# A cross-attention and Fourier FFN kernel: the FFN matrix built without folding the rows of W, its first sum over a quarter of the columns

## The chip, the core and the metric

The kernel runs on one NeuronCore of a Trainium2 chip. Its engines have a queue of instructions each and meet through semaphores: TensorE (matmuls; PE in the profile, PEld its weight loads), VectorE (DVE), ScalarE (ACT), GpSimd (POOL) and SyncE (SP), which here issues DMAs. The metric is the time of one execution on the device in microseconds (us). Before the change its median is 541.05 us over 3 runs (540.98 to 541.4).

## The reference

The input x has 2 x 2048 rows of 512. Each row goes through cross-attention (16 heads of 32, 128 keys per batch) and then through a linear layer that is given in the frequency domain:

```
x = x + attention(layernorm(x), ctx, mask) @ wo + bo
score = (q k^T / sqrt(32)) * mask;  score = -1e9 where score == 0;  softmax
w = complex(w_freq_real, w_freq_imag)          # 512 x 512
y = real(ifft(fft(layernorm(x)) @ w)) + bias
x = x + y
```

The two transforms and w are linear, so the second layer is one real matrix M (512 x 512), found once per call: M[n, m] is 1/512 times a sum over cosines and sines of n with the rows of w and of cosines and sines of m with its columns. All arithmetic is float32.

## The kernel before

The 4096 rows of x are 8 groups of 512, each of four tiles of 128 rows. Group i, tile t is a slot: scores of 16 heads (128 x 128 each), softmax in two halves of eight heads, transposes of the weights, and between them a part of another group's work, so that TensorE always has a matmul to do: queries of the next group (`q`), context (`c`) and projection (`o`) of the last, FFN (`y`) of the last or the one before. The order of all queues is written out by hand: every engine takes its instructions in the program's order. Groups 1 to 7 run in a regular pattern of slots; group 0 has a prologue of its own, up to about 97 us with the first slot of group 1, in which M is also made. The change touches this prologue and the first slots of group 1.

The steps that the change and the prediction speak of:

- `relative` (L234) subtracts a row's first element, `query_statistics` (L209 to L214) takes mean and variance on VectorE and the inverse deviation on GpSimd, `query_norm` (L217, VectorE) normalizes in place, `query_transposes` (L186 on TensorE, L188 on ScalarE) turns the tile. The rows of group n are prepared while group n - 1 or n - 2 is in its slots.
- `Queries` (L200) is a chain of four matmuls of 512 columns (384 for the rest of group 0), evicted by ScalarE (L293) in `evict`.
- `Softmax`: `masked` (L334: scores times mask, VectorE), `maxima` (L341 turns zero scores into the masked value, L343 takes the minima, L344 scales them; VectorE), `exponentials` (eight L350 on ScalarE), `divided` (the reciprocal L362 on VectorE, the multiplication L363 on GpSimd).
- `transposed_weights` (L380 on TensorE) turns weights of four heads into one bank; ScalarE (L387) or, where it is told to, VectorE (L385) copies them out.
- `Values` (L200, evicted by L584 on VectorE) makes v of one batch.
- The matrix M. Its two inputs wr and wi (real and imaginary part of w) are loaded to two tiles. `FoldRows` uses the symmetry of cosine and sine in the rows: a matmul with the flipped identity (`flip`, L614) mirrors a block of 128 rows, and VectorE adds it to and subtracts it from its mirror image (L621, L624), row 0 and row 256 apart (L623, L626). There are four folds, two each for wr and wi. `fold_columns` does the same with columns, on GpSimd (L645, L646), into `cols`. `Mirrored` then sums over 257 cosines and 255 sines (L685) and builds the 512 outputs out of the two halves with an add and a subtraction (L706, L707): four times as `h` (into `half`) and four times as `m` (into `m_ffn`). What belongs to the first row comes in as a bias (`first_rows`: a transpose, L669, of rows that small DMAs, L663, have gathered).

PSUM, where TensorE writes, has three pools of two tiles: scores (`ps_sc`), transposes (`ps_tp`) and chains (`ps_mm`, used by queries, values, folds, h, m, context and projections). A chain's first matmul waits until the chain before the last one has been evicted. In SBUF, wr and wi lie in the two buffers that hold the residual rows of x later, and the cosines and sines in one of the buffers for transposed weights. The order of the prologue's calls stands at the foot of the builder, from `evict_biases, evict_keys = keys()` on.

Of the kernel before, what the change touches and what calls it, by code (L numbers as in the profile page):

```python
# [22 lines left out]
def kernel(  # L23
# [76 lines left out]
    flip = const_tile([P, P], "flip")  # L100
    nc.vector.tensor_copy(flip, ident[:, P - 1 :: -1])
# [55 lines left out]

    wr = big_tile("x", 2, "wr")
    wi = big_tile("x", 2, "wi")
    row0 = const_tile([1, 2, D], "row0")  # L160
    nc.sync.dma_start(row0[:, 0, :], wf_re[0:1, :])
    nc.sync.dma_start(row0[:, 1, :], wf_im[0:1, :])
    nc.sync.dma_start(wr[:, :HC, :], chunks(wf_re[1 : HD + 1, :]))
    nc.sync.dma_start(wr[:, HC:, :], chunks(wf_re[HD:, :]))
    nc.sync.dma_start(wi[:, :HC, :], chunks(wf_im[1 : HD + 1, :]))
    nc.sync.dma_start(wi[:, HC:, :], chunks(wf_im[HD:, :]))
# [4 lines left out]
    nc.sync.dma_start(dft[:, :HC, :], chunks(dft_cos[HD:, :]))  # L171
    nc.sync.dma_start(dft[:, HC:, :], chunks(dft_sin[HD:, :]))
# [23 lines left out]
    def chain(name, lhs, rhs, width=D, between=()):  # L196

        ps = ps_mm.tile([P, D], FP, tag="mm", name=name)[:, :width]
        for c in range(NC):
            nc.tensor.matmul(  # L200
                ps, lhs(c), rhs(c), start=(c == 0), stop=(c == NC - 1)
            )
            if c == HC - 1:
                call(between)
        return ps
# [69 lines left out]
    class Queries:  # L275


        def __init__(self, i, g, first=0):
            self.i, self.g, self.first = i, g, first

        def pe(self):
            i, g = self.i, self.g
            if i not in qTs:
# [5 lines left out]
                width=GQ - self.first * P,  # L289
            )  # L290
# [307 lines left out]
    m_ffn = const_tile([P, NC, D], "m_ffn")  # L598
    half = big_tile("pt", 6, "half")
    cols = big.tile([P, 4, HC, HD], FP, tag="cT", bufs=1, name="cols")  # L600

    class FoldRows:
# [3 lines left out]
        def __init__(self, name, t, other, sign, c):  # L606
            self.name, self.t, self.other, self.sign = name, t, other, sign
            self.c = c

        def pe(self):  # L610

            t, c = self.t, self.c
            self.low = ps_mm.tile([P, D], FP, tag="mm", name=f"low_{self.name}_{c}")
            nc.tensor.matmul(  # L614
                self.low, flip, t[:, HC - 1 - c, :], start=True, stop=True
            )

        def evict(self):
            t, c = self.t, self.c
            total, high = t[:, HC - 1 - c, :], t[:, HC + c, :]  # L620
            nc.vector.tensor_tensor(total, self.low, high, ALU.add)  # L621
            if c == 0:
                nc.vector.tensor_copy(total[0:1, :], high[0:1, :])  # L623
            nc.vector.tensor_tensor(high, high, self.low, ALU.subtract)  # L624
            if c == 0:
                nc.vector.tensor_scalar(  # L626
                    high[0:1, :], row0[:, self.other, :], self.sign, None, ALU.mult
                )

        on_vector = True  # L630

    def fold_columns():


        up, down = slice(HD + 1, D), slice(HD - 1, 0, -1)
        rp, rm, ip, im = wr[:, :HC, :], wr[:, HC:, :], wi[:, :HC, :], wi[:, HC:, :]
        for k, (x1, x2, op, first) in enumerate(
            (
                (rp[:, :, up], rp[:, :, down], ALU.add, rp[:, :, HD : HD + 1]),
                (im[:, :, up], im[:, :, down], ALU.add, im[:, :, HD : HD + 1]),  # L640
                (ip[:, :, down], ip[:, :, up], ALU.subtract, rp[:, :, 0:1]),
                (rm[:, :, up], rm[:, :, down], ALU.subtract, im[:, :, 0:1]),
            )
        ):
            nc.gpsimd.tensor_tensor(cols[:, k, :, 1:], x1, x2, op)  # L645
            nc.gpsimd.tensor_copy(cols[:, k, :, 0:1], first)  # L646

    def cols_of(what, g):
        return lambda i: cols[
            :,  # L650
            2 * what + i // HC,
            HC - 1 - i if i < HC else i - HC,
            g * P : (g + 1) * P,
        ]
# [11 lines left out]
    def first_rows(name, rows, scale):  # L666
# [4 lines left out]
        nc.scalar.mul(add, ps, scale)  # L671
        return add

    class Mirrored:
# [3 lines left out]
        def __init__(self, name, lhs, dst, scale):  # L678
            self.name, self.lhs, self.dst, self.scale = name, lhs, dst, scale

        def pe(self):
            ps = ps_mm.tile([P, D], FP, tag="mm", name=self.name)
            self.even, self.odd = ps[:, : HD + 1], ps[:, HD + 1 :]
            for i in range(NC):
# [3 lines left out]
                    dft[:, i, : HD + 1] if i < HC else dft[:, i, 1:HD],  # L688
# [4 lines left out]
        def evict(self, add, eng=nc.gpsimd):  # L693
            low, high = self.dst[:, 1:HD], self.dst[:, D - 1 : HD : -1]
            nc.scalar.activation(
                self.dst[:, : HD + 1],
                self.even,
                AF.Identity,
                bias=add,
                scale=self.scale,  # L700
            )
            odd = self.odd
            if eng is nc.gpsimd:
                odd = work.tile([P, HD - 1], FP, tag="odd", name=f"odd_{self.name}")
                nc.scalar.mul(odd, self.odd, self.scale)
# [112 lines left out]
    for t in range(TG):  # L818
        relative(1, t, nc.gpsimd if t < 2 else nc.vector)
    query_statistics(1, 0, TG - 1)  # L820
    for g in range(NC):
        first_queries(0, g)
# [4 lines left out]
    folds = [  # L827
        FoldRows(name, w, other, sign, c)
# [397 lines left out]
```

## Time and profile before

| what | value |
|---|---|
| median of 3 runs | 541.05 us (540.98 to 541.4) |
| the profiled execution | 541.23 us, its span 539.0 us |
| granted TensorE clock, mean | 1.000 |
| TensorE idle, 20 to 99 us | 4.6 of 79 us |
| VectorE busy, 20 to 99 us | 64.9 of 79 us |
| ScalarE busy, 20 to 99 us | 53.8 of 79 us |
| GpSimd busy, 20 to 99 us | 50.4 of 79 us |
| start of the scores of slots (0,1), (0,2), (0,3), (1,0) | 36.45, 50.36, 63.96, 80.88 us |

A group of instructions is one source line on one engine with one pair of tiles; behind its name stand the number of instructions, the busy time in us, the mean of one in ns, and the idle time before them with what ended it. A float32 matmul is two instructions on TensorE, a transpose is one. In the chain of work that ended last, each piece has its start and length in us. In the list of waits, the numbers are the total in us, how often, and the longest. Times are from the span's start.

### The profile page before, as it was taken

The page shows a single profiled execution, that of the slowest core. Times are in us where ns is not written, and L with a number is a line of the kernel's source. Part 1 is how long each engine was busy: PE and PEld are TensorE (multiplying, and loading weights), DVE is VectorE, ACT ScalarE, POOL GpSimd, SP SyncE. Part 2 cuts the span into 40 slices and gives each one's busy share as a digit, 9 for nine tenths or more (in the row PEclk, how much of TensorE's full clock was granted, in tenths as well). Part 3 has the DMA queues.
Part 4 walks back from the last instruction along what each step waited for, and adds up shares of the span by engine and source line. Part 5 has one row for each costly group of instructions (what it writes and reads, how often), then busy time and mean ns, then how long its engine had stood idle before and what let it go on. Part 6 is the DMA issues. An engine that isn't in the chain of part 4 may idle for free.

```text
span 539.0 us, 8776 instructions
## 1 busy us (share of the span) xinstructions
PE 526.0 (98%) x3005; PEld 293.4 (54%) x3005; DVE 437.2 (81%) x617; ACT 342.3 (64%) x1299; POOL 330.0 (61%) x268
## 2 busy tenths in 40 slices
PE   8979999999999999999999999999999999999897
PEld 7745567455545555455545555455545554455344
DVE  4698888799987998879887998879967898987251
ACT  3376786676677676666677676666676667666210
POOL 3246768935895459735895459735764466866450
PEclk9999999999999999999999999999999999999999
DMA  8960203000510015000610015000312001201002
GB/s 309 385 224 0 76 4 99 1 0 2 195 41 2 19 52 184 0 21 1 196 40 0 21 51 184 1 21 0 118 41 76 23 20 48 91 1 60 19 0 79
DMA packets 22992, 36.49 MB, mean 68 GB/s; under 512 B 2202, under 2 KB 6562, under 8 KB 22948
## 3 DMA queue, kind: packets, MB, share of 16 engines
q1 hardware_dynamic: 22260, 34.75, 18.7%
q10 hardware_dynamic: 688, 1.18, 0.6%
q8 instruction: 24, 0.39, 0.3%
q14 instruction: 20, 0.16, 0.1%
HBM read 27.53 MB, written 8.39 MB: 67 GB/s over the span
## 4 chain that ended last, share of the span: by engine, by line
PE 83%; DVE 10%; ACT 3%; POOL 2%; issue 1%; POOLq 0%; ACTq 0%; DVEq 0%
PE o L200 20%; PE q L200 16%; PE y L200 16%; PE tpw L380 9%; PE c L402 6%; PE sc L315 5%; PE tp_f L186 3%; PE tp_a L186 3%; ACT w L350 2%; DVE w L341 2%; DVE w L334 2%; DVE nmax L343 2%; POOL w L363 1%; PE k L547 1%; PE v L200 1%; DVE st_a L209 1%
## 5 line engine op out<-in xcount | busy, mean ns | idle before, releaser
L350 ACT ACTIVATE w<-w,nmax 128x128 f32<-128x128 f32 x512 | 198.3, 395 | 16.0 <-DVE nmax L344 15.0
L363 POOL TENSOR_TENSOR w<-w,rden 128x1024 f32<-128x1024 f32 x64 | 123.9, 1935 | 84.9 <-DVE rden L362 69.3
L200 PE MATMUL o<-wo,cT 128*128 128x512 f32 x256 | 115.3, 594 | 0.0
L200 PE MATMUL q<-xnT,wq 128*128 128x512 f32 (+1 forms) x256 | 112.0, 582 | 2.6 <-ACT qT L293 1.5
L200 PE MATMUL y<-m_ffn,nT 128*128 128x512 f32 x248 | 112.0, 594 | 0.2 <-DVE x L503 0.2
L387 ACT COPY pt<-tpw 128x512 f32<-128x512 f32 x120 | 64.3, 587 | 60.0 <-PE tpw L380 60.0
L350 ACT ACTIVATION_READ_ACCUMULATOR w<-w,nmax 128x1 f32 x512 | 99.2, 194 | 0.0
L341 DVE SCALAR_TENSOR_TENSOR w<-w 128x1024 f32<-128x1024 f32 x64 | 88.8, 1387 | 0.9
L334 DVE TENSOR_TENSOR w<-sc,mask 128x1024 f32<-128x1024 f32 x64 | 77.5, 1212 | 13.9 <-PE sc L315 13.6
L343 DVE TENSOR_REDUCE nmax<-w 128x8 f32<-128x1024 f32 x64 | 78.1, 1220 | 2.2
L380 PEld LDWEIGHTS tpw<-ident,w 128*128 128x128 f32 x496 | 57.7, 141 | 33.6 <-issue 29.3
L200 PEld LDWEIGHTS q<-xnT,wq 128*128 128x128 f32 x256 | 46.3, 190 | 48.6 <-issue 40.2
L200 PEld LDWEIGHTS o<-wo,cT 128*128 128x128 f32 x256 | 46.2, 190 | 47.5 <-issue 46.1
L200 PEld LDWEIGHTS y<-m_ffn,nT 128*128 128x128 f32 x248 | 44.6, 190 | 44.6 <-issue 43.8
L380 PE MATMUL tpw<-ident,w 128*128 128x128 f32 x496 | 65.2, 273 | 2.0 <-POOL w L363 1.0
L458 POOL TENSOR_TENSOR x<-x,bf 128x512 f32<-128x512 f32 x32 | 50.4, 1576 | 15.0 <-DVE norm_f L217 15.0
L213 POOL TENSOR_SCALAR rstd_f<-mv_f 128x1 f32<-128x1 f32 x32 | 18.1, 564 | 67.0 <-DVE mv_f L210 67.0
L418 POOL TENSOR_TENSOR x<-x,bo 128x512 f32<-128x512 f32 x32 | 46.9, 1494 | 0.0
L234 POOL TENSOR_SCALAR rel<-rows 128x512 f32<-128x512 f32 x26 | 42.2, 1638 | 1.4 <-PE tp_a L186 1.4
L315 PEld LDWEIGHTS sc<-kT,qT 32*128 32x128 f32 x1024 | 31.5, 186 | 15.1 <-issue 12.8
L188 ACT COPY nT<-tp_f 128x512 f32<-128x512 f32 x29 | 16.9, 583 | 34.3 <-PE tp_f L186 34.2
L362 DVE RECIPROCAL rden<-den 128x8 f32<-128x8 f32 x64 | 12.6, 197 | 31.9 <-ACT w L350 31.7
(99 smaller groups left out, 550.6 us busy)
## 6 DMA issues: line engine op xcount, KB each, us to landing
rows<-in_x_dram SPq DMA_DIRECT2D x32, 256.0 KB, 4.3
x<-in_x_dram SPq DMA_DIRECT2D x32, 256.0 KB, 5.1
out_dram<-x SPq DMA_DIRECT2D x31, 256.0 KB, 2.0
mask<-in_mask_Bx1xSxS_fk_dram SPq DMA_DIRECT2D x8, 256.0 KB, 5.8
wk<-in_L_xattn_wk_w_dram ACTq DMA_DIRECT2D x2, 512.0 KB, 6.3
wq<-in_L_xattn_wq_w_dram SPq DMA_DIRECT2D x1, 1024.0 KB, 7.8
wr<-n_L_ffn_w_freq_real_dram SPq DMA_DIRECT2D x2, 512.0 KB, 5.2
wi<-n_L_ffn_w_freq_imag_dram SPq DMA_DIRECT2D x2, 512.0 KB, 7.4
```

What stands on the lines that cost most here:

```text
L200: nc.tensor.matmul(ps, lhs(c), rhs(c), start=(c == 0), stop=(c == NC - 1))
L234: eng.tensor_scalar(d, xt, xt[:, 0:1], None, ALU.subtract)
L315: nc.tensor.matmul(sc[r // 2][:, r % 2, g, :], qTs[i][rows, g, t * P : (t + 1) * P], kT[rows, g, b * K : (b + 1) * K], start=True, stop=True,)
L334: nc.vector.tensor_tensor(self.w, self.sc.rearrange("p r g k -> p (r g) k"), self.mrow, ALU.mult)
L341: nc.vector.scalar_tensor_tensor(w, w, 0.0, w, ALU.is_equal, ALU.subtract)
L343: nc.vector.tensor_reduce(self.nmax, w, AX.X, ALU.min)
L350: nc.scalar.activation(w[:, h, :], w[:, h, :], AF.Exp, bias=self.nmax[:, h : h + 1], scale=-UNIT, accum_out=self.den[:, h : h + 1],)
L363: nc.gpsimd.tensor_tensor(w, w, rden.unsqueeze(2).to_broadcast([P, HH, K]), ALU.mult)
L380: nc.tensor.transpose(ps[:, r, :], ws[r // 2].w[:, (r % 2) * NC + g, :], ident)
L387: nc.scalar.copy(dst, ps)
L418: nc.gpsimd.tensor_tensor(xs[:, t, :], xs[:, t, :], bo, ALU.add)
L458: nc.gpsimd.tensor_tensor(xt, xt, bf, ALU.add)
```

## The change

The rows of W are no longer folded. `FoldRows`, `flip`, the row-0 loads and `fold_columns` go. `add_columns` and `subtract_columns` fold columns of all 512 rows on GpSimd (1020 elements a partition in place of 510). The first sum, `First`, runs over all rows, but makes a quarter of the output's range: cosines and sines of even and of odd rows apart, which `first` (GpSimd) and `second` (VectorE) put together to the 512 outputs. Its weights are every second column. wr and wi lie so that a partition holds two neighbouring rows, and the cosine and sine table is loaded in four parts. The factor 1/512 moves from m to the first sum, and only m has first rows to add.

The order of the prologue is new: `subtract_columns(0)` and `(1)` stand with the divisions of slot (0,0); `query_norm` of group 1 stands behind both divisions; the last `relative` of group 1 stands on VectorE between the halves; values are made a slot earlier; two of the four query chains of group 0 use transpose banks; the first sums are spread over slots (0,1) and (0,3), the last of m goes into slot (1,1); the query chain 0 of group 2 comes before group 1; two copies of weights (first half of slot (0,2)'s) move to VectorE; the loads of rows and masks come earlier in the program.

```diff
-    flip = const_tile([P, P], "flip")
-    nc.vector.tensor_copy(flip, ident[:, P - 1 :: -1])
...
+    def parted(rows):
+        return rows.rearrange("(p c) n -> p c n", c=HC)
...
-    nc.sync.dma_start(row0[:, 0, :], wf_re[0:1, :])
-    nc.sync.dma_start(row0[:, 1, :], wf_im[0:1, :])
...
+    for to, of in ((wr, wf_re), (wi, wf_im)):
+        for rs, cs in halves_of_rows:
+            nc.sync.dma_start(to[:, cs, :], parted(of[rs, :]))
...
+    for rs, cs in halves_of_rows:
+        nc.sync.dma_start(cosines[:, cs, :], parted(dft_cos[rs, : HD + 1]))
+        nc.sync.dma_start(sines[:, cs, :], parted(dft_sin[rs, 1:HD]))
...
-    def chain(name, lhs, rhs, width=D, between=()):
+    def chain(name, lhs, rhs, width=D, between=(), spare=False):
+        pool, tag = (ps_tp, "tp") if spare else (ps_mm, "mm")
+        ps = pool.tile([P, D], FP, tag=tag, name=name)[:, :width]
...
+    up, down = slice(HD + 1, D), slice(HD - 1, 0, -1)
+    def add_columns(k):
+        t = (wr, wi)[k]
+        nc.gpsimd.tensor_tensor(cols[:, k, :, 1:], t[:, :, up], t[:, :, down], ALU.add)
+        nc.gpsimd.tensor_copy(cols[:, k, :, 0:1], t[:, :, HD : HD + 1])
+    def subtract_columns(k):
+        t, other = ((wr, wi), (wi, wr))[k]
+        a, b = ((up, down), (down, up))[k]
+        nc.gpsimd.tensor_tensor(t[:, :, up], t[:, :, a], t[:, :, b], ALU.subtract)
+        nc.gpsimd.tensor_copy(t[:, :, HD : HD + 1], other[:, :, 0:1])
+    QD = HD // 2
+    class First:
+        def __init__(self, what, g):
...
+            if what == 0:
+                self.lhs = [lambda c, k=k: cols[:, k, c, g::HC] for k in range(2)]
+            else:
+                self.lhs = [lambda c, t=t: t[:, c, HD + g :: HC] for t in (wi, wr)]
         def pe(self):
+            ps = self.ps = ps_mm.tile([P, D], FP, tag="mm", name=self.name)
+            at = 0
+            for k, table, odd, n in (
+                (0, cosines, 0, QD + 1),
+                (0, cosines, 1, QD),
+                (1, sines, 0, QD - 1),
+                (1, sines, 1, QD),
+            ):
+                for b in range(2):
+                    c = b * HC + odd
+                    nc.tensor.matmul(
+                        ps[:, at : at + n], self.lhs[k](c), table[:, c, :n],
+                        start=(b == 0), stop=(b == 1),
+                    )
+                at += n
         def evict(self):
+            self.t = work.tile([P, D], FP, tag="parts", name=f"t_{self.name}")
+            nc.scalar.mul(self.t, self.ps, 1.0 / D)
+        def first(self):
...
+            for k, op in enumerate((ALU.add, ALU.subtract)):
+                nc.gpsimd.tensor_tensor(u[:, k, :, : QD - 1], even, odd, op)
+                nc.gpsimd.tensor_tensor(
+                    self.dst[:, k * HD : k * HD + QD + 1 : QD],
+                    t[:, : QD + 1 : QD], t[:, QD + 1 :: D - QD - 2], op,
+                )
+        def second(self):
...
+            nc.vector.tensor_tensor(d[:, :, 1:QD], cos, sin, ALU.add)
+            nc.vector.tensor_tensor(d[:, ::-1, HD - 1 : QD : -1], cos, sin, ALU.subtract)
...
-    for t in range(TG):
+    for t in range(TG - 1):
         relative(1, t, nc.gpsimd if t < 2 else nc.vector)
     query_statistics(1, 0, TG - 1)
+    for k in range(2):
+        add_columns(k)
...
-    rest = [Queries(0, g, 1) for g in range(NC)]
+    rest = [Queries(0, g, 1, g >= HC) for g in range(NC)]
...
     w[0].maxima()
+    relative(1, TG - 1, nc.vector)
+    load_rows(2)
+    load_mask(1)
     w[0].exponentials()
     w[1].masked()
     run(rest[1])
     w[1].maxima()
     w[1].exponentials()
+    subtract_columns(0)
+    w[0].divided()
+    query_statistics(1, TG - 1, TG)
+    run(rest[2])
+    run(rest[3])
+    values[0].pe()
+    w[1].divided()
     for t in range(TG):
         query_norm(1, t)
-    w[0].divided()
-    run(folds[0])
-    w[1].divided()
-    run(folds[1])
+    values[0].evict()
+    subtract_columns(1)
...
     w = begin(0, 1)
...
+    h[0].pe()
+    transposed_weights(0, 0, HC, NC)
     w[1].exponentials()
+    h[0].evict()
     w[0].divided()
-    run(folds[2])
+    query_statistics(2, 0, 2)
+    run(q[0])
     w[1].divided()
-    run(folds[3])
+    h[0].first()
+    h[0].second()
+    load_rows(3)
     w = begin(0, 2)
...
     w[0].divided()
+    query_norm(2, 0)
+    query_norm(2, 1)
+    q[3].pe()
     w[1].divided()
+    query_norm(2, 2)
+    query_norm(2, 3)
+    q_last, q = q[3], [Queries(2, g) for g in range(NC)]
     w = begin(0, 3)
     w[0].masked()
+    q_last.evict()
+    h[1].pe()
+    h[1].evict()
+    h[1].first()
     w[0].maxima()
+    h[2].pe()
+    h[2].evict()
+    h[2].first()
+    transposed_weights(0, 2, 0, HC, nc.vector)
     w[0].exponentials()
     w[1].masked()
+    h[1].second()
+    h[2].second()
+    h[3].pe()
+    h[3].evict()
+    h[3].first()
     w[1].maxima()
+    h[3].second()
+    load_residual(0)
     rows_m = load_first_rows("rows_m", [x.lhs(HC)[0:1, :] for x in m])
+    for t in range(TG):
+        query_transposes(2, t)
     transposed_weights(0, 2, HC, NC)
     w[1].exponentials()
     w[0].divided()
+    relative(3, 0, nc.gpsimd)
+    run(q[0])
     w[1].divided()
+    relative(3, 1, nc.gpsimd)
     load_mask(2)
     w = begin(1, 0)
...
+    def last_of_m():
+        m[3].pe()
+        m[3].evict(add[:, 3:4])
```

## The prediction

> **What bounds the kernel now.** I read the page first (busy time, shares of the chain), then the chain in order of time for the first 100 us, then what TensorE waited for, then two stretches of the timelines of VectorE and GpSimd.
>
> The page: TensorE is busy for nearly the whole span and holds 83% of the chain. So over the whole kernel a matmul taken away is time won.
>
> ```profile
> PE 526.0 (98%) x3005; PEld 293.4 (54%) x3005; DVE 437.2 (81%) x617; ACT 342.3 (64%) x1299; POOL 330.0 (61%) x268
> PE 83%; DVE 10%; ACT 3%; POOL 2%; issue 1%; POOLq 0%; ACTq 0%; DVEq 0%
> ```
>
> All that the change touches lies before 112 us, though, and there the chain (start, length, what) looks different. Between 20 and 82 us it runs mostly through the softmax on VectorE and its exponentials on ScalarE, with TensorE between:
>
> ```profile
> 31.69 3.19 ACT w L350 x16
> 34.88 0.47 ACT qT L293
> ...
> 35.40 1.12 PE low_wr L614 x2
> ...
> 48.71 0.88 PE low_wi L614 x2
> ...
> 53.49 1.15 DVE w L334
> ...
> 66.81 1.10 DVE w L334
> ...
> 75.36 3.70 PE q L200 x8
> ```
>
> So here two queues are almost equally long. TensorE's own waits up to 140 us (total, times, longest) are small; these make 3.9 of the 4.4 us that it stands still between 20 and 99 us (the last one lies behind 81):
>
> ```profile
> PE q L200 <- ACT qT L293: 1.5, 1, 1.5
> PE q L200 <- ACT odd_half L705: 1.0, 1, 1.0
> PE low_wr L614 <- ACT qT L293: 0.9, 1, 0.9
> PE tpw L380 <- POOL m_ffn L707: 0.5, 1, 0.5
> ```
>
> The line that decides my forecast is this pair from the timelines of VectorE and GpSimd (start, length):
>
> ```profile
> 31.57 1.91 DVE L217 TENSOR_SCALAR rel<-rel,mv,rstd 128x512 f32<-128x512 f32 x4
> 110.46 2.53 DVE L217 TENSOR_SCALAR rel<-rel,mv,rstd 128x512 f32<-128x512 f32 x2
> 110.61 2.09 POOL L363 TENSOR_TENSOR w<-w,rden 128x1024 f32<-128x1024 f32 x1 [2.73 <-DVE rden L362]
> ```
>
> Four normalizations take 1.91 us while GpSimd is idle; two take 2.53 us when one division of GpSimd falls between them. The two engines take turns: the division, asked for at 110.61, waits for the first normalization, and the second waits for the whole division. The same is seen for the masking step L341: 1.23 us alone, 1.83 us at 54.66 against L645, 2.00 us at 67.94 against L363.
>
> **The change, part by part.** TensorE's work first. From the chain and the groups:
>
> ```profile
> L614 PE MATMUL low_wr<-wr,flip 128*128 128x512 f32 x4 | 2.1, 618 | 0.9 <-ACT qT L293 0.9
> L200 PE MATMUL q_first<-xnT,wq 128*128 128x128 f32 x32 | 3.7, 275 | 0.0
> L645 POOL TENSOR_TENSOR cols<-wr 128x510 f32<-128x510 f32 x2 | 2.5, 1269 | 0.0
> ```
>
> - The four flips go: 8 passes of 0.43 us (a 512-wide chain of 8 passes lasts 3.44) = -3.44. One transpose of first rows goes: -0.17.
> - The first sums have as many columns as before, in 16 passes of about 128 instead of 8 of 256. q_first runs 32 such passes in 3.57 us, 0.112 each: 1.79 a sum against 1.73, four times: +0.25. Sum of TensorE's work: -3.36.
> - Their weights are now read with a step of two elements, which no row shows. Bounds: nothing (weight loads last 186 to 192 ns in every shape of the trace), or twice the pass, 64 x 0.112 = +7.1. I take nothing, the nearest rows. The dear end would fall mostly into TensorE's new waits (below), so I carry it as +2 at most. [...]
>
> VectorE loses the folds (34.51 to 38.3 and 49.61 to 53.4, 7.4 us with waits). It gains eight adds of about 0.41 in `second`, at a pitch of 0.34 (rows L706 and L707 on VectorE): 2.7; and two copies of weights, 1.28.
>
> GpSimd's four column sums now have 1020 elements instead of 510: two-input rows give 0.73 (255), 1.27 (510), so 2.34 each; lower end 1.90 (the division's 1024 elements). They move from 54 us to three places: `add_columns` twice when wr and wi have landed (about 19 and 23), `subtract_columns(0)` after that, `subtract_columns(1)` after the second division. `first` adds two adds of 0.73 and two of two elements (0.19, the row of L646, to 0.6, L213): 1.85 a sum.
>
> Costed at nothing, with cover: the cosine and sine loads in shorter rows (read from about 47, landed near 30); rows of group 2 (the loads now wait for `relative(1,3)` near 28, land by 36, are read near 42); rows of group 3 (earlier by 30 us); the residual load (waits for the last first sum near 74 in place of 62.7, is read after 102); mask 2 (needed near 140); `rows_m` (issued near 84.5, landing 1.7 later, read near 91: this cover is 4 us, and m[0]'s eviction and the chain of m wait if it goes). GpSimd's `relative(2)` (4 x 1.58) now stands behind `subtract_columns(1)`, to 48, and is read near 50.6; two of `relative(3)` stand before and behind the last division of group 0, to 91, whose transposes come near 92.6. The two query chains in transpose banks take away the 1.5 and 0.9 us waits above.
>
> Now the order, in this profile's own time. `relative(1,3)` and three statistics no longer stand before the first masking, so that can start when its scores end (21.5, not 23.1); the column sums of wi, 23 to 28, take turns with L341 and the small L344 there. I let the two cancel (-1.6 to +1.6): the second exponentials end at 34.9 as now.
>
> 1. `query_norm(1)` moves from 31.57 behind the second division's reciprocal (35.1). There it meets the division and `subtract_columns(1)` in turn: 4 x 0.54 + 1.90 + 2.34 + small copies = 6.6, to 41.7. Group 1's transposes, which TensorE reaches at 37.5, wait for them: 3.9. Then the value eviction (0.6): the masking of (0,1) starts at 42.3, not 38.3.
> 2. A half of the softmax is 3.8 on VectorE (1.22 + 1.24 + 1.25 + 0.1). Transposed weights are copied at 47.1, then two times eight exponentials (3.1 each) with two copies between: 54.3. Reciprocal, division 1.9, `first` 1.85, and VectorE waits, idle, for `second` of h[0], which stands before the next masking: 54.3 + 0.1 + 1.9 + 1.85 + 0.8 = 59.0, not 53.5. The value eviction behind both halves holds TensorE 1.5.
> 3. Slot 2: 59.0 + 3.8 + 1.2 + 1.6 (two statistics) + 2.6 = 68.1, exponentials to 71.2. Four normalizations take turns with two divisions: 68.2 + 4 x 0.54 + 2 x 1.90 = 74.3, the masking of (0,3); now 66.8. h[2] needs the bank of q[3], evicted behind those exponentials: 1.8.
> 4. Slot 3: 74.3 + 3.8 + 0.4 (turns) = 78.5; the copies of weights now on VectorE end behind that (79.1, 79.7), and group 2's transposes need their banks: 3.1. The next two need ScalarE's copies, behind eight exponentials and an eviction: 78.5 + 3.1 + 0.6 + 0.5 = 82.7, a wait of 2.6 + 0.3. Two transposes of rows and two of weights (0.44 each), then q[0]: 82.7 + 1.9 + 3.44 = 88.0, where the scores of (1,0) start, not 80.88: +7.1.
>
> TensorE's books agree: before that point -1.8 of work (-3.36, one query chain ahead +3.44, m[0] and its row transpose behind -1.9), 3.9 of old waits gone (4.4 less the last), new waits 3.9 + 1.5 + 1.8 + 3.1 + 2.9 = 13.2: +7.5. After it TensorE has one chain of 1.73 more and one of 3.44 fewer: 7.3 - 1.7 = +5.6. But VectorE enters group 1 seven us late and is busy there 4.9 of 5 us:
>
> ```profile
> 130.00:135.00 5.00, 5.00 (x19) 2.64 (x18) 4.93 (x7) 2.06 (x8) 0.93 (x3) 1.00 0.00 0
> ```
>
> (columns: PE, PEld, DVE, ACT, POOL, clock.) If it can't catch up, TensorE waits for normalizations and context evictions: 0 to 3.9 (three normalizations that meet a division lose 1.3 each: the one at 124.28 lasts 1.84, not 0.54), I take 1.4. Sum +7.0. After 140 us nothing differs. The profiled execution took 541.23 (span 539.0 and 2.2 around it), 0.2 over the median; on the median 541.05 the sum is 548.0.
>
> A rule weighed: the clock was granted in full in every 5-us window from 5 to 150 us, with TensorE idle for 1.5 at a time. My new waits are up to 3.9, and two of them have only transposes between. [...]
>
> **Rivals.**
> - *Faster.* VectorE, rid of the folds, keeps ahead, and the old waits go: -3.36 - 4.4, with some 1.5 of new waits: 534.8. Its one mechanism is that the turns of steps 1 to 4 don't happen or hide; it decides when TensorE's new waits up to 112 us stay under 7.8 us. For it: VectorE has 2.5 us less to do. Against: the 2.53 us pair, and that `second` in step 2 waits for GpSimd in any case.
> - *Turns cost less.* Queued normalizations run back to back ahead of GpSimd. Step 1's wait of 3.9 goes; of the later ones only 0.6, since banks, copies and `second` hold TensorE still: 7.0 - 4.5 = +2.5, 543.5. Against: at 110.86 the division got in between.
> - *Slower still.* Strided weights at half speed: 7.1 on TensorE, of which I leave 2 on the path, since h[1] to h[3] lie beside waits of 7.8; and two-element adds at 0.6 in step 2, +0.8: 550.8.
> - *No change.* Saved work and new waits cancel: 541.
>
> **Numbers.** Mine 0.56, turns cost less 0.19, slower still 0.12, faster 0.09, no change 0.04. Slower by over 0.2% (1.1 us, about what a measurement of this kernel can tell from none): 0.56 + 0.19 + 0.12 = 0.87; same 0.04; faster 0.09. The likeliest's own range: 546 to 550 (step 1's -1.6 to +1.6, later waits 0 to 3.9). The range for 8 in 10 takes in the second rival's 543.5 with 1 us of room and half of the third: 542.5 to 551.
>
> **What would show it.** In the profile after: no L614 matmuls; first-sum passes 0.112 us apart (right) or 0.2 (strided price); `query_norm(1)` lasting over 5 us instead of 1.91 (right), or about 2 (wrong); VectorE idle near 55 to 58 before `second`; waits of TensorE on normalizations, on weight copies of VectorE and on ScalarE near 40, 50, 70, 79 and 82, 11 to 15 us in all; the scores of (1,0) near 88. If they start before 80, my forecast is wrong.

## The result and the profile after

The changed kernel takes 549.25 us (median of 4 executions, 548.05 to 551.6) against 541.22 for the kernel before on the same chip: a ratio of 1.0152, 95% interval 1.0125 to 1.0179. It is 8.0 us slower; 548.0 was forecast, with a range of 542.5 to 551. The time is inside the range, and most of the mechanism is as told, but that the sum came out so near is luck, since errors cancel: up to the scores of (1,0), TensorE's waits are a third shorter than forecast (8.7 us, not 13.2), and two things that the sum left out (work that I forgot, and a clock that was cut) fill most of the gap.

The profiled execution took 548.05 us, span 545.9. The page's busy line and the shares of the chain: TensorE is as busy as before (526.0 then), the span is 6.9 longer, and the chain's 83% on TensorE have become 76%.

```profile
PE 525.7 (96%) x3028; PEld 295.3 (54%) x3028; DVE 439.4 (80%) x612; ACT 341.1 (62%) x1293; POOL 342.6 (63%) x278
PE 76%; DVE 12%; ACT 5%; DMA 4%; POOL 1%; issue 1%; ACTq 0%; POOLq 0%; DVEq 0%
```

TensorE's waits from 20 to 160 us (total, times, longest):

```profile
PE tp_a L190 <- DVE rel L223: 2.8, 3, 1.5
PE tp_a L190 <- ACT xnT L192: 2.5, 2, 2.3
PE tp_a L190 <- DVE pt L392: 1.7, 1, 1.7
PE tp_f L190 <- DVE norm_f L223: 1.7, 1, 1.7
PE half L653 <- ACT qT L300: 1.2, 1, 1.2
PE q L206 <- DVE v L591: 1.1, 1, 1.1
PE c L409 <- DVE cT L419: 0.8, 1, 0.8
```

The two waits for ScalarE's query evictions (1.5 by a query chain, 0.9 by a fold) are gone from the list. In their place stand the places that the prediction named: normalizations, the value eviction, the bank of the last query chain, the copies of weights, and ScalarE's copies of the turned tiles. VectorE's timeline (start, length) shows where they come from. The group of four at 34.62 is the one that took 1.91 us before; the two pairs of 2.53 us look like the pair of before on which the forecast rested:

```profile
34.62 5.68 DVE L223 TENSOR_SCALAR rel<-rel,mv,rstd 128x512 f32<-128x512 f32 x4
40.82 1.21 DVE L341 TENSOR_TENSOR w<-sc,mask 128x1024 f32<-128x1024 f32 x1
56.86 0.42 DVE L685 TENSOR_TENSOR half<-u_half 128x254 f32<-128x254 f32 x1 [3.44 <-POOL u_half L672]
57.53 1.22 DVE L341 TENSOR_TENSOR w<-sc,mask 128x1024 f32<-128x1024 f32 x1
66.80 2.53 DVE L223 TENSOR_SCALAR rel<-rel,mv,rstd 128x512 f32<-128x512 f32 x2
70.23 2.53 DVE L223 TENSOR_SCALAR rel<-rel,mv,rstd 128x512 f32<-128x512 f32 x2
72.69 1.21 DVE L341 TENSOR_TENSOR w<-sc,mask 128x1024 f32<-128x1024 f32 x1
```

The maskings (L341 here) of slots (0,1), (0,2) and (0,3) start at 40.82, 57.53 and 72.69. Before, they were L334 and started earlier:

```profile
38.31 1.22 DVE L334 TENSOR_TENSOR w<-sc,mask 128x1024 f32<-128x1024 f32 x1
53.41 1.22 DVE L334 TENSOR_TENSOR w<-sc,mask 128x1024 f32<-128x1024 f32 x1
66.73 1.17 DVE L334 TENSOR_TENSOR w<-sc,mask 128x1024 f32<-128x1024 f32 x1
```

The difference grows from 2.5 to 4.1 to 6.0 us: each of the first three steps puts VectorE later. TensorE's timeline around the worst place (in brackets the idle time ahead and what ended it), and the stretch of 5 us from 80 (busy times of PE, PEld, DVE, ACT and POOL, then the granted clock):

```profile
77.36 1.25 PE L190 MATMUL tp_a<-ident,rel 128*128 128x128 f32 x8 [1.75 <-DVE pt L392]
80.94 1.82 PE L190 MATMUL tp_a<-ident,rel 128*128 128x128 f32 x8 [2.33 <-ACT xnT L192]
82.58 1.97 PE L387 MATMUL tpw<-ident,w 128*128 128x128 f32 x8
84.34 3.71 PE L206 MATMUL q<-xnT,wq 128*128 128x512 f32 x8
87.98 1.17 PE L322 MATMUL sc<-kT,qT 32*128 32x128 f32 x32
...
80.00:85.00 5.00, 4.06 (x18) 3.47 (x19) 3.68 (x8) 3.54 (x7) 3.63 (x5) 0.66 0.20 55
```

The scores of (1,0) start at 87.98 (forecast 88.0). But the granted clock is 0.66 in this stretch, after two waits (1.75 and 2.33 us) with only eight transposes between, and eight transposes take 1.82 us that took 1.25 just before. I call such a stretch a cut of the clock.

TensorE's books (its busy and its idle time up to a point), first of before and then of after, from 20 us to the scores of (1,0) and from there to those of (1,3) (length, PE busy, then the other engines):

```profile
20.00:80.88 60.88, 56.81 (x325) 34.40 (x324) 52.45 (x81) 41.00 (x162) 33.81 (x29) 1.00 0.32 111
80.88:126.84 45.96, 45.43 (x286) 26.52 (x286) 39.09 (x50) 33.23 (x127) 33.45 (x27) 1.00 0.10 29
```

```profile
20.00:87.98 67.98, 59.30 (x363) 37.82 (x361) 52.64 (x70) 41.59 (x159) 44.95 (x40) 0.97 0.35 116
87.98:133.83 45.85, 42.64 (x270) 24.95 (x270) 38.78 (x51) 31.32 (x125) 33.80 (x26) 1.00 0.00 1
```

Up to the scores of (1,0) TensorE has 2.5 us more busy time (59.30 - 56.81) and 4.6 more idle (8.68 - 4.07), together the 7.1. After that it is busy 2.8 less and idle 2.7 more, together nothing. The span ends 6.9 later.

### The profile page after: what moved, and what is told of

Same layout as the page of the kernel before. It is cut to its first block, busy times and chain, and to the rows that moved or that the text cites. A ratio compares the mean times of both kernels' runs of the same rounds, so it can differ in the third digit from the quotient of the medians.

```text
span 545.9 us, 8809 instructions
## 1 busy us (share of the span) xinstructions
PE 525.7 (96%) x3028; PEld 295.3 (54%) x3028; DVE 439.4 (80%) x612; ACT 341.1 (62%) x1293; POOL 342.6 (63%) x278
## 4 chain that ended last, share of the span: by engine, by line
PE 76%; DVE 12%; ACT 5%; DMA 4%; POOL 1%; issue 1%; ACTq 0%; POOLq 0%; DVEq 0%
PE o L206 18%; PE y L206 16%; PE q L206 15%; PE tpw L387 8%; PE c L409 6%; PE sc L322 5%; ACT w L357 4%; DVE w L348 3%; PE tp_f L190 3%; DVE nmax L350 2%; DVE w L341 2%; PE tp_a L190 2%; DMA wi<-n_L_ffn_w_freq_imag_dram 1%; PE m L717 1%; POOL w L370 1%; DMA wk<-in_L_xattn_wk_w_dram 1%
## 5 line engine op out<-in xcount | busy, mean ns | idle before, releaser
L348 DVE SCALAR_TENSOR_TENSOR w<-w 128x1024 f32<-128x1024 f32 x64 | 87.9, 1373 | 0.9
L341 DVE TENSOR_TENSOR w<-sc,mask 128x1024 f32<-128x1024 f32 x64 | 77.5, 1213 | 13.8 <-PE sc L322 12.0
L240 POOL TENSOR_SCALAR rel<-rows 128x512 f32<-128x512 f32 x26 | 45.3, 1754 | 1.5 <-PE tp_a L190 1.5
```

The costliest lines, as they stand in the source:

```text
L240: eng.tensor_scalar(d, xt, xt[:, 0:1], None, ALU.subtract)
L341: nc.vector.tensor_tensor(self.w, self.sc.rearrange("p r g k -> p (r g) k"), self.mrow, ALU.mult)
L348: nc.vector.scalar_tensor_tensor(w, w, 0.0, w, ALU.is_equal, ALU.subtract)
```

## The experiments

My theory: VectorE's queue comes late because its normalizations take turns with GpSimd (steps 1 and 3) and because `second` stands idle in front of a masking (step 2), and TensorE waits behind it. The main rival: the loss is in TensorE's own work, the 16 short passes and the weights with a step of two elements. A third question is what the cut clock costs and where it comes from. The first four kernels ran on a chip where the kernel before takes 541.22, as it did in the result; the other eight on another (before: 541.56 and 541.67), where e9 is the changed kernel itself. Ratios are to the kernel before.

**e1 to e4: the three steps undone, one at a time and together.** e1 (step 1):

```diff
     values[0].pe()
-    w[1].divided()
     for t in range(TG):
         query_norm(1, t)
+    w[1].divided()
     values[0].evict()
```

> Edit: in slot (0,0) the four normalizations of group 1 stand ahead of the second division's reciprocal instead of behind it; the work is the same. Mine (VectorE's queue is late by turns with GpSimd, TensorE follows): the four normalizations last about 1.9 us instead of 5.68, the masking of (0,1) starts near 37.4 instead of 40.82, the 2.3 us that TensorE waits for normalizations and their copies near 36 to 41 go to under 0.5; 2.3 to 3.4 us faster than the changed kernel: 546 to 547. Rival (the time went into TensorE's own work, the short passes and strided weights): the group gets shorter, the end moves by under 0.5 us: 549.

Measured: 547.0 us (545.76 to 548.77), ratio 1.0109 (1.0082 to 1.0136), so 2.2 under the changed kernel by medians and by the profiled executions (545.8 to 548.05), the lower end of what was expected. VectorE's and TensorE's timelines of e1:

```profile
34.91 1.91 DVE L223 TENSOR_SCALAR rel<-rel,mv,rstd 128x512 f32<-128x512 f32 x4 [2.57 <-POOL rstd L220]
...
37.41 1.21 DVE L341 TENSOR_TENSOR w<-sc,mask 128x1024 f32<-128x1024 f32 x1
...
37.94 1.14 PE L190 MATMUL tp_a<-ident,rel 128*128 128x128 f32 x8 [0.29 <-ACT xnT L192]
```

Four normalizations in 1.91 us, as in the kernel before, and TensorE waits 0.29 where it waited 2.3. Step 1 is right. It is not worth the whole 3.4 by which the masking moved, since in slot (0,1) subtract_columns(1) then meets the softmax, whose second masking starts only 2.9 earlier (41.79, then 44.66).

e2 (step 2):

```diff
     h[0].first()
-    h[0].second()
...
     w[0].maxima()
+    h[0].second()
```

> Edit: second of h[0] (two adds on VectorE) stands behind the first half's maxima of slot (0,2) instead of ahead of its masking. Mine: the 3.44 us in which VectorE stands idle before it go, the masking of (0,2) starts near 54 instead of 57.53; 2.5 to 3.4 us faster than the changed kernel: 546 to 547. Rival (VectorE's lateness is hidden, TensorE's work decides): under 0.5 us: 549.

Measured: 547.42 us (545.84 to 548.57), ratio 1.0113 (1.0088 to 1.0138): 1.8 faster than the changed kernel by both measures, under the 2.5 to 3.4 expected. The masking of (0,2) starts at 54.43, as expected, and the gap of 3.44 is gone. But this profile has a cut clock at 40 us that the profile of the changed kernel has not (0.76 from 40 to 45), with nearly the same waits ahead of it (0.61 and 1.48; 0.60 and 1.48 there); part of the gain is given back there.

e3 (step 3):

```diff
+    for t in range(TG):
+        query_norm(2, t)
     w[0].divided()
-    query_norm(2, 0)
-    query_norm(2, 1)
     q[3].pe()
     w[1].divided()
-    query_norm(2, 2)
-    query_norm(2, 3)
```

> Edit: in slot (0,2) the four normalizations of group 2 stand ahead of both divisions instead of two behind each. Mine: they last about 1.9 us in one group instead of 2.53 twice, the masking of (0,3) starts near 70 instead of 72.69; 1.5 to 3 us faster than the changed kernel: 546.5 to 548. The division starts 1.9 us later, which nothing but the transposes of those weights, far behind, needs. Rival (TensorE's work decides): under 0.5 us: 549.

Measured: 547.92 us (547.15 to 550.36), ratio 1.0138 (1.0111 to 1.0165), 1.3 faster by medians and 0.7 by the profiled executions, under the 1.5 to 3 expected. With four executions each, the intervals of e1, e2 and e3 all overlap that of the changed kernel (1.0125 to 1.0179), so no end time proves one of the three moves by itself; what is firm is that each brings its masking forward. Of the three, e3 is the least certain. Its profile has the same extra cut at 40 us (0.74). The four normalizations take 1.91 us in one group, and the masking of (0,3) starts at 71.31 instead of 72.69.

e4 is all three:

> The three moves together. Mine: TensorE's new waits of steps 1 to 3 go, 7 to 9 us together; what is left are the copies behind exponentials in step 4 and the later waits, and TensorE has 3.4 us less work than the kernel before: 539 to 542.5, scores of (1,0) near 80. If the granted clock drops near 80 because of TensorE's waits, this falls away with them. Rival (strided weights and short passes hold TensorE): 545 or more, and the scores of (1,0) not ahead of 84.

Measured: 540.01 us (10 executions, 539.44 to 543.3), ratio to before 0.9987 (0.9973 to 1.0001): 9.2 under the changed kernel, and not to be told from the kernel before. The scores of (1,0) start at 81.66. The three moves alone gave 2.25, 1.83 and 1.33, 5.4 together; all three give 9.2. What is over fits the clock, though no run shows that part by itself: nine of the ten executions have a mean granted clock of 0.999 or 1.000 and take 539.4 to 541.4; the changed kernel's four have 0.991 to 0.996. The one of e4 with 0.993 is the profiled one, with 543.3. Its TensorE has these waits left, and the clock is cut behind the first, and once more in the last slots (0.77 from 500 to 505 us, 0.89 from 505 to 510):

```profile
74.14 1.14 PE L190 MATMUL tp_a<-ident,rel 128*128 128x128 f32 x8 [1.88 <-ACT xnT L192]
95.57 1.07 PE L409 MATMUL c<-pt,v 128*32 128x512 f32 x8 [0.81 <-DVE cT L419]
112.55 0.63 PE L190 MATMUL tp_a<-ident,rel 128*128 128x128 f32 x4 [0.72 <-DVE rel L223]
126.96 0.63 PE L190 MATMUL tp_f<-ident,norm_f 128*128 128x128 f32 x4 [1.68 <-DVE norm_f L223]
...
75.00:80.00 5.00, 4.80 (x16) 2.71 (x15) 1.95 (x5) 4.39 (x17) 4.06 (x6) 0.66 0.23 64
```

TensorE's work is the same in e4 as in the changed kernel. So the rival falls: the loss was order, not work.

**e9, the changed kernel on the second chip**, as the measure for e5 to e12:

> The changed kernel itself, as the measure for the next three on the same chip. 549 to 550; its executions spread over 2 to 3 us, as they did (548.05 to 551.6), since the clock is cut at one or two places.

Measured: 551.57 us (551.39 to 551.9), ratio 1.0177 (1.0159 to 1.0195). It is not spread at all here: all four executions have a mean clock of 0.991, and the profile shows two cuts, at 40 us (0.66 from 40 to 45) and behind 80 us, the second twice as long (0.67 from 80 to 85 and 0.65 from 85 to 90), and a slower first softmax (e12).

**e5 and e10: the clock.** e5 fills the second place, e10 both, with matmuls whose result nobody reads (`keep_busy(ps, n)`: n matmuls of 512 columns into a spare bank). In e10:

```diff
     for t in range(TG):
+        if t < 3:
+            keep_busy(idle, (1, 1, 2)[t])
         query_transposes(1, t)
...
     for t in range(TG):
+        if t % 2 == 0:
+            keep_busy(idle, 2)
         query_transposes(2, t)
```

> Edit: two matmuls of 512 columns (1.7 us) that nobody reads are put on TensorE ahead of group 2's first transposes and again between its second and third, where it stood still for 1.75 and 2.33 us in the changed kernel. If the halved clock near 80 to 84 us comes from TensorE's idleness: granted clock 1.00 there, the eight transposes and the eight turned weights behind the wait take about 1.1 us each instead of 1.82 and 1.97, and the kernel is about 1.7 us faster, 547.5. If the clock is cut for another reason: 0.66 again from 80 to 85, and 549.

> The changed kernel with unread matmuls of 512 columns in the waits at both places: four of 0.86 us among group 1's transposes (36 to 41 us) and four among group 2's (75 to 82). If idleness of TensorE cuts the clock: 1.00 in every window from 20 to 150 us, mean clock 0.999 or more in nearly all executions, 1.7 to 3 us faster than e9_changed_again and with less spread, 547. If something else cuts the clock: 0.50 to 0.66 again, and the same time or up to 1 us more.

Measured: e5 550.09 us (547.25 to 550.86), 1.5 under e9; e10 549.67 us (548.99 to 549.86), 1.9 under e9, every execution at a mean clock of 0.999 or 1.000. Both expectations named 547 or so; the differences are as expected, the level is this chip's. Two stretches of e9 and then of e10:

```profile
40.00:45.00 5.00, 4.05 (x15) 3.20 (x16) 4.97 (x6) 1.90 (x4) 5.00 (x5) 0.66 0.21 54
85.00:90.00 5.00, 5.00 (x18) 3.30 (x17) 1.72 (x5) 4.05 (x13) 4.06 (x6) 0.65 0.20 58
```

```profile
40.00:45.00 5.00, 4.38 (x20) 2.66 (x20) 4.93 (x7) 1.66 (x3) 5.00 (x5) 1.00 0.17 54
85.00:90.00 5.00, 4.90 (x28) 2.64 (x32) 1.60 (x6) 4.74 (x21) 4.07 (x5) 1.00 0.21 58
```

And the work behind the second place in e10, which answers to the 1.82, 1.97 and 3.71 us shown above:

```profile
83.77 1.14 PE L190 MATMUL tp_a<-ident,rel 128*128 128x128 f32 x8 [0.60 <-ACT xnT L192]
85.10 1.15 PE L387 MATMUL tpw<-ident,w 128*128 128x128 f32 x8 [0.19 <-ACT xnT L192]
```

Adding 6.9 us of useless matmuls (8 of 0.86) to TensorE made the kernel faster by 1.9. So at these two places it is TensorE's idleness that cuts the clock (0.66 and 0.65 in the stretches of e9, 1.00 in those of e10). In the changed kernel's profile the cut at the second place costs about 1.6 us, as the work behind it is on the path (1.82 + 1.97 - 1.14 - 1.15 = 1.5, and 0.1 of q). In e5's profile the clock is full there and the same work takes 1.14 and 1.15, as expected, but at the first place, which e5 does not fill, the clock is 0.50 from 40 to 45 us and 0.86 from 45 to 50. What a cut at the first place costs stays open: e10 is 0.4 faster than e5 by medians, but e5's own executions go from 547.25 (mean clock 0.999) to 550.86 (0.993), and no run separates that cut from the first softmax (e12).

**e6: turns or place?**

```diff
     values[0].evict()
-    subtract_columns(1)
```

> Leaves subtract_columns(1) out (GpSimd, 2.18 + 0.39 us), so wi goes unfolded into the first sums of h[2] and h[3]; no instruction on VectorE or TensorE changes. If VectorE's normalizations take turns with GpSimd: the four last 4 x 0.54 + 1.90 = about 3.9 us instead of 5.68, the masking of (0,1) starts near 39 instead of 40.82, about 1.8 us faster, 547.4. If the normalizations are long only because they start behind the second division: 5.7 again and 549.

Measured: 549.28 us (548.36 to 549.81), 2.3 under e9; the normalizations of e6 start and last

```profile
36.25 3.64 DVE L223 TENSOR_SCALAR rel<-rel,mv,rstd 128x512 f32<-128x512 f32 x4
```

3.64 us (5.68 in e9), and the masking of (0,1) starts at 40.41 instead of 42.70. The second normalization lasts 0.53 instead of 2.21: a column difference that is only on GpSimd (2.18 us), and that nothing waits for in this slot, costs VectorE 1.68 us there. They take turns. The rest of the 2.04 us is in the fourth normalization, 0.54 instead of 0.91. In e9, as in the changed kernel, that one runs beside the first `relative` of group 2 on GpSimd (L240, the subtraction of a row's first element), which in e6 starts later.

With L240 the turn can go the other way. Here L348, the step of the softmax that turns zero scores into the masked value, and an L240 of e9:

```profile
43.94 1.23 DVE L348 SCALAR_TENSOR_TENSOR w<-w 128x1024 f32<-128x1024 f32 x1
44.32 2.28 POOL L240 TENSOR_SCALAR rel<-rows 128x512 f32<-128x512 f32 x1
```

L348 takes its time alone, though the L240 before this one (42.77 to 44.34) was still running when it started. The next L240 starts behind L348 and takes 2.28 us instead of 1.56.

**e12: the first softmax.**

```diff
-    for k in range(2):
-        add_columns(k)
+    add_columns(0)
...
-    subtract_columns(0)
     w[0].divided()
```

> Leaves add_columns(1) and subtract_columns(0) out, which run on GpSimd beside the first softmax (the first sums of h[0] and h[1] read wr's column sums twice, h[2] and h[3] wr unfolded). In the changed kernel they stretch L348 once to 2.12 (or 3.14) us and L351 to 0.94 or 1.09. Mine: all four are 1.22 and 0.17, the second masking starts at about 25.6 instead of 26.34 to 28.9, the second exponentials end 1.5 to 3 us earlier, and the kernel is 1.5 to 3 us faster than e9_changed_again. Rival (there is room in front of the second reciprocal): under 0.5 us.

Measured: 547.79 us (546.96 to 548.08), 3.8 under e9, more than expected. L348 and the scaling of the minima (L351) in the first softmax, and the masking (L341) behind them, first of e9 and then of e12:

```profile
23.22 3.19 DVE L348 SCALAR_TENSOR_TENSOR w<-w 128x1024 f32<-128x1024 f32 x1
27.70 1.10 DVE L351 TENSOR_SCALAR nmax<-nmax 128x8 f32<-128x8 f32 x1
29.11 1.21 DVE L341 TENSOR_TENSOR w<-sc,mask 128x1024 f32<-128x1024 f32 x1
```

```profile
23.17 1.22 DVE L348 SCALAR_TENSOR_TENSOR w<-w 128x1024 f32<-128x1024 f32 x1
25.68 0.17 DVE L351 TENSOR_SCALAR nmax<-nmax 128x8 f32<-128x8 f32 x1
26.16 1.22 DVE L341 TENSOR_TENSOR w<-sc,mask 128x1024 f32<-128x1024 f32 x1
```

A scaling of eight elements a row, 0.17 us of work, takes 1.10: a column difference on GpSimd runs from 26.43 to 28.78. Of the 3.8 us, 2.95 are in VectorE's rows (the second masking at 26.16, not 29.11; the masking of (0,1) at 39.75, not 42.70). The rest fits the clock, though no run shows it by itself: e9's profile has a cut at 40 us, and e12's has none there.

Which of the two engines starts first is a toss-up. In e9 the column sum of wi starts on GpSimd at 22.99, when wi has landed, ahead of L348, which then lasts 3.19. In the changed kernel's profile it starts at 23.01, behind an L348 that had begun at 22.57 and is done in 1.23, and it is the sum that gets longer (2.99 in place of 2.35). All eleven profiles that have both steps are of one kind or the other: in six L348 takes 1.23 and the sum 2.84 to 3.24; in five the sum takes 2.34 or 2.35 and L348 2.70 to 3.37 (in e5 too the sum starts first, at 22.74, and L348 at 23.03). It is not the chip alone: e11, on the second one, is of the first kind (L348 takes 1.23 at 23.04, the sum 3.21).

The changed kernel's second masking starts at 26.34, e9's at 29.11. At the masking of (0,1) only 1.9 of these 2.8 us are left (40.82 and 42.70), as the second L348 takes 2.12 in the first order and 1.23 in the other, and 0.65 were there already at the first masking (21.31 and 21.96). The two profiled executions are 3.3 us apart; the rest fits e9's additional cut and its longer one, which no run shows by itself either.

**e7: the weights with a step of two.** e4_all_three with

```diff
-                self.lhs = [lambda c, k=k: cols[:, k, c, g::HC] for k in range(2)]
+                self.lhs = [lambda c, k=k: cols[:, k, c, g * P : (g + 1) * P] for k in range(2)]
```

and the same for h[2] and h[3].

> The three moves of e4_all_three, and the weights of the first sums are 128 neighbouring columns instead of every second (so the four sums are of the wrong columns); compared with e4_all_three. If a step of two elements costs nothing: passes 0.118 us apart as before, 540.0. If it costs something that is in the 0.118: down to the 0.112 of q_first, 64 x 0.006 = 0.4 us less at most.

Measured: 541.58 us (540.45 to 542.94) on the second chip, ratio 0.9996 (0.9984 to 1.0008); e4 did not run there, so the times say nothing on this and the rows decide. One group of the first sums (count, busy, mean ns of one), first of e4 and then of e7:

```profile
L653 PE MATMUL half<-dft,wr 128*128 128x128 f32 x8 | 1.3, 282 | 0.0
```

```profile
L653 PE MATMUL half<-dft,wr 128*128 128x128 f32 x8 | 1.2, 275 | 0.0
```

275 ns is what q_first has (neighbouring weights, 128 columns). The step of two costs some 6 ns a pass, 64 x 6 = 0.4 us in all: not the 7.1 of the dear end, and not quite the nothing that the prediction took. The rival "slower still" falls with it; its other half too, as a two-element add (L674) in step 2 takes 0.20 us.

**e8: one part of the change alone.** The kernel before with this line (and `chain` and `Queries` changed to take a bank of the other pool):

```diff
-    rest = [Queries(0, g, 1) for g in range(NC)]
+    rest = [Queries(0, g, 1, g >= HC) for g in range(NC)]
```

> The kernel before with one part of the change alone: two of the four query chains of group 0 in transpose banks. TensorE's waits of 1.5 (q) and 0.9 (low_wr) on ScalarE's evictions near 31 to 36 go. What is late next is the softmax on VectorE, which the folds follow: they start up to 1.7 earlier and so does the masking of (0,1). Mine: 1 to 2 us faster than before, 539.2 to 540.2. Rival (group 1's transposes wait for these banks instead, or the masking of (0,1) waits for GpSimd): within 0.5 us, 541.

Measured: 540.48 us (10 executions, 540.27 to 540.9) against 541.56, ratio 0.9977 (0.9968 to 0.9987): 1.1 faster, in the lower part of what was expected, and the one kernel here that is shown to beat both. The waits of 1.5 and 0.9 are gone; 0.94 (scores of (0,1) for the query evictions behind the exponentials) and 0.75 (a query chain for a fold) stand in their place, so TensorE's waits from 20 to 99 us sum to 3.4 us instead of 4.4, which is the gain. The masking of (0,1) does not come earlier, as was expected: it starts at 38.59 (38.31 in the kernel before, on the first chip).

**e11: more moves.** e4_all_three, and

```diff
+    values[1].evict()
     w[1].masked()
     w[1].maxima()
-    values[1].evict()
...
     q_last.evict()
+    query_transposes(2, 0)
+    query_transposes(2, 1)
...
-    transposed_weights(0, 2, 0, HC, nc.vector)
+    query_transposes(2, 2)
+    query_transposes(2, 3)
...
+    transposed_weights(0, 2, 0, HC)
...
-    for t in range(TG):
-        query_transposes(2, t)
...
+        if norms_first:
+            call(on_b)
         halves[0].divided()
```

> e4_all_three with four more moves: v's second eviction ahead of the second masking of (0,1); group 2's transposes ahead of the exponentials of (0,3); the two copies of weights back on ScalarE; the normalizations of slots (1,1) and (1,2) ahead of the reciprocal. Mine: of the waits that e4_all_three still has, 1.88 (tp_a), 1.68 (tp_f) and 0.72 (tp_a) shrink to under 2 together and no wait is long enough to cut the clock: 1 to 2 us faster than e4_all_three, 538 to 539.5, faster than the kernel before. Rival (VectorE is as long as TensorE in group 1 whatever the order): 540 to 541.

Measured: 542.1 us (10 executions, 540.7 to 543.58), ratio 1.0004 (0.9991 to 1.0017): not faster than before, so the expectation failed. Of the three waits that it was to shrink, 1.68 and 0.72 have become 0.81 and 0.74, but 1.88 is 2.12 at another place. Still it is ahead of the kernel before until the last slots (the first `tpw_last` at 497.12 against 498.38). There the clock is cut, in code that the change does not touch. The stretch of before and then of e11:

```profile
500.00:505.00 5.00, 4.17 (x36) 1.85 (x36) 1.38 (x2) 1.77 (x4) 3.90 (x4) 1.00 0.14 52
```

```profile
500.00:505.00 5.00, 4.32 (x25) 1.48 (x28) 1.06 (x2) 1.27 (x3) 2.64 (x3) 0.66 0.00 0
```

The waits there are the same in both (0.28 or 0.29, 0.68 and 0.68), and the cut costs 1.6 us (the four transposes and the context chains behind them take 1.04 and 4.95 instead of 0.66 and 3.69). Nine of e11's ten executions have a mean clock of 0.993 to 0.997; of the 12 of before on that chip, two have 0.996 and take 543.1. Whether a cut follows waits of this size is decided by something that no run here shows.

## Why the prediction was right, and where it was not

- **The direction and the sum.** The forecast was +7.0 us on the profiled execution and 6.8 came (548.05 against 541.23). By medians it is +8.0; the other three executions have a lower mean clock (0.991 to 0.994; 0.996 in the profiled one). That 6.8 is so near 7.0 is luck, as the books of step 4 show.
- **Step 1**: right in its mechanism (e1, e6), too large. The turns came as told: the first normalization lasts 2.26 (the division), the second 2.21 (the column sum), the third 0.53. The fourth lasts 0.91, but not by the small copy, which ends at 39.06, before this one starts at 39.39: beside it runs an L240 (39.04 to 40.92). But the group starts at 34.62, not 35.1, and lasts 5.68, not 6.6 (the column sum takes 2.18 instead of 2.34, and one normalization follows the other after 0.45), so it ends at 40.3 instead of 41.7. TensorE's wait was put at 3.9 and is 2.3 (0.60 + 1.48 + 0.20), because the first tiles' transposes run between the turns.
- **The first softmax, "I let the two cancel (-1.6 to +1.6)"**: true for the profiled execution (the second half's exponentials end near 34.4; 34.9 before). In e9, with the other order, they end near 36.3, at the upper end of that range. I had seen that the two meet, and not that which starts first is a toss-up.
- **Step 2**: the idle 3.44 us in front of `second` are there, the masking of (0,2) is at 57.53 (59.0 less the 1.5 of step 1), the value eviction holds TensorE 1.10 (1.5). e2 confirms it.
- **Step 3**: two pairs of 2.53, the masking at 72.69 (74.3; the terms of that sum give 74.2), h[2]'s wait 1.22 (1.8). e3 points the same way, with less certainty.
- **Step 4**: the scores of (1,0) start where the forecast had them, and for partly wrong reasons. The two waits are 1.75 and 2.33 (3.1 and 2.6). The step that failed is "TensorE's books agree": the new waits up to there are 8.7 us, not 13.2, and the work is not -1.8 but +2.5. Left out of it were the four transposes of group 2, which now stand ahead of these scores (16 of 0.109, +1.7), the step of two (+0.4 over the sum) and the cut clock (+1.6). The remaining 0.5 is not placed. (The reading that weight loads last 186 to 192 ns in every shape was also wrong, without harm to the sum: in the trace of before they last 141 ns for transposes and 108 for the context.)
- **After the scores of (1,0)**: work -2.8 instead of -1.7 (the same transposes, 1.7, are missing here; 0.6 the other way is not placed), waits 2.7 more instead of 1.4, inside the bounds 0 to 3.9. The two errors cancel. The price named for a normalization that meets a division, 1.3, was nearly right: behind the waits of 0.72 and 1.68 stand normalizations of 2.12 and 1.85 us instead of 0.54.
- **The clock, weighed and left out.** The sum has no term for a cut clock: I went by the rows, in which TensorE had stood still for at most 1.5 at a time under a full clock (1.00). Here that was the wrong guide: 0.66 over 5 us is 1.7 us lost, 1.6 by e10, and by the mean clocks (0.996 to 0.991 over 546 us) an execution loses 2 to 5 us of full clock. Waits of 1.75 and 2.33 with eight transposes between are enough, and at 0.61 and 1.48 the clock was cut in e2 and not, with 0.60 and 1.48, in the changed kernel's profile.
- **The rivals.** "Turns cost less" is wrong in its mechanism: the turns are there. "Slower still" is excluded by e7: its 7.1, twice the pass, was an estimate that no run shows, and the runs show 0.4. "Faster" put the decision at 7.8 us of new waits up to 112 us; the changed kernel has 9.5 up to there, and with the three moves undone 540.0 is reached and no more: e4's profile still has waits of 1.88, 0.81, 0.72 and 1.68.

## What to carry to other kernels

Before a step is moved to a free place in VectorE's queue, look at what GpSimd does in that place: 1.9 us of normalizations became 5.7 between a division and a column sum, and one line moved back brought 2.2 us. When TensorE's books are made for a point of the program, list every instruction that crosses that point, those of untouched helpers too; mine agreed with the end only because what I forgot and what I overpriced had the same size. And price a wait of TensorE with the clock behind it: waits of 1.75 and 2.33 us with eight transposes between cost 1.6 us more than themselves, and a filler of unread matmuls gave that back.

## What the runs showed of the hardware

- Idle TensorE time cut its clock to a half, after waits of 1.75 and 2.33 us with transposes between: in the profile after it is 0.64 from 81.0 to 81.5 us, 0.50 from 81.5 to 84.5, 0.94 from 84.5 to 85.0 and 1.00 again from there. In e9 (0.67 from 80 to 85 us, 0.65 from 85 to 90) and e5 (0.50 from 40 to 45, 0.86 from 45 to 50) about twice as much clock was lost. In e11 the clock was cut after waits of 0.29, 0.68 and 0.68 too (0.66 from 500 to 505 us), where the kernel before kept 1.00. With unread matmuls in the waits it stayed at 1.00 (e10).
- VectorE's normalizations, L348 and even an eight-element scaling wait for a GpSimd addition or subtraction of two tiles to end: 0.53 us became 2.21 (e6, e9), 1.22 became 3.19 and 0.17 became 1.10 (e12, e9). The subtraction of a row's first element on GpSimd (L240) is different: one that is already running holds L348 up little or not at all (1.23 us at 43.94 in e9, 1.42 at 41.65 in e6), lengthens a normalization by some 0.4 (0.91 instead of 0.54), and one that starts behind L348 waits for it (2.28 us instead of 1.56). Why the two kinds differ is not shown.
- The same program has two first softmaxes, 1.9 us apart at the masking of (0,1) in two profiles (0.65 of it there before the softmax starts), depending on which starts first, a GpSimd sum whose load has just landed or L348 (22.99 and 23.22 us in e9, 23.01 and 22.57 in the changed kernel's first profile).
